# Sorting's constants ahead of the adjacency's transfers, node sums in two column tiles of the array, degrees within the table's chain

## The chip, the cores and the metric

The kernel runs on one core of one Trainium2 chip. The metric is the device time of one execution in microseconds (us), median of several runs. Profiles are of one execution each. In them PE is TensorE's matmuls, PEld its weight loads, DVE VectorE, ACT ScalarE, POOL GpSimd, SP SyncE. A releaser in square brackets after a line says how long the engine was idle before it and what ended that.

The change touches only what comes before the layer's last stage, 320.9 us in the kernel before. The rest, from the first product of that stage ("first mix product") to the end, is untouched.

## The reference, cut to what matters

Four graph layers follow one another; only the first is concerned. For 8 samples, 2048 nodes, 64 groups (H) and 64 features:

```python
h = x @ W
s = leaky_relu(h @ a_node, 0.2)
alpha = softmax(where(H.T > 0, s[:, None, :], NEG))        # over the nodes of a group
agg = einsum('ben,bnf->bef', alpha, h)                      # the node sums
beta = sigmoid((h @ a_gn)[:, None, :] + (agg @ a_ge)[:, :, None])
all_he = elu(beta * h + (1 - beta) * agg)                   # per node and group
deg = maximum(adj.sum(-1), 1.0)                             # degrees
industry = einsum('nm,bmf->bnf', adj / deg, x @ W_ind)
se = attn_scores(elu(agg))                                  # tanh(f @ fcW + fcb) @ av
g = einsum('bne,benf->bnf', softmax(where(H > 0, se, NEG)), all_he)
out = softmax-weighted sum of industry and g
```

The kernel sorts the nodes by their number of groups, so that a tile of 128 sorted nodes needs only as many "slots" (one group of each node at a time) as its fullest node.

## The kernel before

Its start has four parts. The 14.7 MB of the adjacency's first fourteen tiles are requested on GpSimd's queue. The sort runs on VectorE with small products on TensorE. The **node loop** makes, for each of 16 node tiles, h, the scores, the node sums in `pagg`, and a row block `st` which is written to HBM (`hs_hbm`) for the later gather in sorted order. The **table's chain** turns `pagg` into the table of groups and the one-hots of the first slots. Then the **slot loop** runs, one product of three passes (`pz`) per slot, with passes over the adjacency as filler: the degrees (`du`), then the layer's neighbour sums (`ug`).

```python
for t in range(NT - XT):                         # 14 of 16 adjacency tiles, 1 MB each
    ahead = min(t + 4, XB - 1)
    tc.keep_in_program_order(nc.gpsimd.tensor_copy(seen_x, xt[ahead][:, 0, 0:1]))
    load_adj(t)                                  # a transfer on GpSimd's queue
# ... only then on GpSimd:
nc.gpsimd.iota(iota, [[1, P]], base=0, channel_multiplier=0, ...)     # the sort's constants
# ... the sort on VectorE, then
nc.gpsimd.dma_start(av_col, ...)                 # and the other small transfers
for t in range(NT):                              # the node loop
    # ph = x tile by weights; seen, lr, e_gn
    st = pa.tile([P, HROW], F32, tag="st", name="st", bufs=5)
    nc.scalar.copy(st[:, BF + 8:], slot[:, t, :])
    # ... VectorE fills st and ex
    nc.scalar.dma_start(hs_hbm[t * P:(t + 1) * P, :], st)
    for k in range(2):
        nc.tensor.matmul(pagg[:, k, ...], lhsT=m_n[:, t, :], rhs=ex[:, k], ...)   # 64 groups
# ... the chain, with 40 of the 64 degree passes within it
def begin(t):                                    # slot loop, per tile
    both = split(hy, hrow[:, 0:BF], "hr", 2, [P, BF], pin=t < 2)      # hrl on VectorE
    # scores of the slots, then
    nc.vector.tensor_reduce(rs, ps[...], AX.X, ALU.add)
    nc.vector.tensor_scalar(rs, rs, 1.0e-30, None, op0=ALU.max)
    nc.vector.reciprocal(rs, rs)
```

Of the kernel before, what the change touches and what calls it, by code (L numbers as in the profile page):

```python
# [49 lines left out]
BINS = 16  # L50
# [6 lines left out]
def tile_gnn_fast(  # L57
# [151 lines left out]
    def staged(name):  # L209
        return hy.tile([P, JT, P], F32, tag="x", name=name, bufs=4)  # L210
# [5 lines left out]
    inv_row = hy.tile([P, N], F32, name="inv_row")  # L216
# [41 lines left out]


# [4 lines left out]
    with tc.tile_pool(name="pa", bufs=1) as pa, tc.tile_pool(name="pa_ps", bufs=1, space=PSUM) as pps:  # L264
# [5 lines left out]
        m_en = [pa.tile([P, HROW], F32, tag="st", name=f"m_en{c}", bufs=5)[0:E, 0:C] for c in range(NCH)]  # L270
# [9 lines left out]
        for t in range(XB):  # L280
            fetch_xt(t)

        bd66 = pa.tile([P, 2, F + 2], F32, name="bd66")
        nc.vector.memset(bd66, 0.0)
        w0t = pa.tile([F, P], F32, name="w0t")
        a2 = pa.tile([F, 2], F32, name="a2")
# [8 lines left out]
        for t in range(NT - XT):  # L295
            ahead = min(t + 4, XB - 1)
            tc.keep_in_program_order(nc.gpsimd.tensor_copy(seen_x, xt[ahead][:, 0, 0:1]))
            load_adj(t)
# [8 lines left out]
        tri = pa.tile([P, P], BF16, name="tri")  # L307
        make_upper_triangular(nc, tri, 1.0, diag=False)
        ones_b = pa.tile([P, P], BF16, name="ones_b")
        nc.vector.memset(ones_b, 1.0)  # L310
        iota = pa.tile([P, P], F32, name="iota")
        nc.gpsimd.iota(iota, [[1, P]], base=0, channel_multiplier=0, allow_small_or_imprecise_dtypes=True)
        row = pa.tile([P, 1], F32, name="row")
        nc.gpsimd.iota(row, [[1, 1]], base=0, channel_multiplier=1, allow_small_or_imprecise_dtypes=True)
        nc.vector.tensor_scalar(m_n, m_n, 0.0, None, op0=ALU.is_gt)
        deg = pa.tile([P, NT], F32, name="deg")
# [4 lines left out]
        oh = pa.tile(bins, BF16, name="oh")  # L321
        nc.vector.tensor_tensor(oh, deg[:, :, None].to_broadcast(bins), i16, ALU.is_equal)
        gt = pa.tile(bins, F32, name="gt")
        nc.vector.tensor_tensor(gt, deg[:, :, None].to_broadcast(bins), i16, ALU.is_gt)
        gts = pa.tile([P, BINS], F32, name="gts")
        nc.vector.tensor_reduce(gts, gt.rearrange("p t b -> p b t"), AX.X, ALU.add)
        gtb = pa.tile([P, BINS], BF16, name="gtb")
# [17 lines left out]
        rank = pa.tile([P, NT], F32, name="rank")  # L345
# [4 lines left out]
        caps = pa.tile([P, BINS], F32, name="caps")  # L350
        for s in range(BINS):
            nc.gpsimd.memset(caps[:, s:s + 1], float(P * SLOT_TILES[s]) if s < len(SLOT_TILES) else 0.0)
        over = pa.tile([P, BINS], F32, name="over")
# [5 lines left out]
        tri_e = pa.tile([E, E], BF16, name="tri_e")  # L359
        make_upper_triangular(nc, tri_e, 1.0, diag=True)  # L360
# [14 lines left out]
        tl = pa.tile([P, NT], F32, name="tl")  # L375
        ge = pa.tile([P, NT, NT], F32, name="ge")
# [7 lines left out]
        q = pa.tile([P, NT], F32, name="q")  # L384
# [4 lines left out]
        val = pa.tile([P, NT, 2, NT], BF16, name="val")  # L389
# [5 lines left out]
        for t in range(NT):  # L395
            ohq = pa.tile([P, P], BF16, tag="ohq", name="ohq", bufs=2)
            nc.vector.tensor_scalar(ohq, iota, q[:, t:t + 1], None, op0=ALU.is_equal)
            nc.tensor.matmul(
                po.rearrange("p i t -> p (i t)"), lhsT=ohq,
                rhs=val[:, t].rearrange("p i t -> p (i t)"), start=t == 0, stop=t == NT - 1,  # L400
            )
        olo = pa.tile([P, NT], F32, name="olo")
# [3 lines left out]
        for dst, v in ((fcb_col, fc_b), (av_col, av)):  # L406
            nc.gpsimd.dma_start(dst, v.rearrange("(n o) -> n o", o=1))
        for t in (fcz, bd_ind):
            nc.gpsimd.memset(t, 0.0)
        for b in range(2):  # L410
            s = slice(b * F, (b + 1) * F)
            nc.gpsimd.dma_start(fcz[s, b, :], fc_w)
            nc.gpsimd.dma_start(bd_ind[s, s], w_ind)
        nc.gpsimd.memset(avz, 0.0)
# [3 lines left out]
        age = pa.tile([E, F], F32, name="age")  # L418
        nc.gpsimd.dma_start(age, bass.AP(tensor=a_ge.tensor, offset=a_ge.offset, ap=[[0, E], [1, F]]))
# [3 lines left out]
        pagg = pps.tile([E, 2, C], F32, tag="agg", name="pagg", bufs=1)  # L423
        G = B // 2
        for t in range(NT):
# [8 lines left out]
            st = pa.tile([P, HROW], F32, tag="st", name="st", bufs=5)  # L434
# [22 lines left out]
            for k in range(2):  # L457
                nc.tensor.matmul(
                    pagg[:, k, 0:G * (F + 1)], lhsT=m_n[:, t, :], rhs=ex[:, k].rearrange("p g c -> p (g c)"),
                    start=t == 0, stop=t == NT - 1,  # L460
                )
# [14 lines left out]

        ones_r = hy.tile([P, P], F32R, name="ones_r")
        nc.gpsimd.tensor_copy(ones_r, ones)
        du = [pph.tile([P, 2, C], F32, tag="ph", name=f"du{g}", bufs=2) for g in range(2)]

        def degrees():
            for t in range(NT):
                for c in range(NCH):
                    mm(
                        du[c // 2][:, c % 2, :], lhsT=ones_r, rhs=adj[t][:, cols(c)],
                        start=t == 0, stop=t == NT - 1,
                    )
                    yield

        degree_passes = degrees()  # L490

        def some_degrees(tiles):
            for _ in range(tiles * NCH):
                next(degree_passes)

        some_degrees(6)


        gv = pagg[:, :, 0:G * (F + 1)].rearrange("p k (g c) -> p k g c", c=F + 1)
        den = pa.tile([E, B], F32, name="den")  # L500
        d3 = den.rearrange("p (k g) -> p k g", k=2)
        nc.vector.tensor_scalar(d3, gv[:, :, :, F], 1.0e-30, None, op0=ALU.max)
        nc.vector.reciprocal(den, den)
        agg = pa.tile([E, B, F], F32, tag="ex", name="agg", bufs=2)
        nc.vector.tensor_tensor(
            agg.rearrange("p (k g) f -> p k g f", k=2), gv[:, :, :, 0:F],
            d3[:, :, :, None].to_broadcast([E, 2, G, F]), ALU.mult,
        )
        tab = pa.tile([E, B, F], F32, tag="st", name="tab", bufs=5)
        tsm = pa.tile([E, 2, B], F32, name="tsm")  # L510
        sc = pa.tile([E, 2, B], F32, name="sc")
        nc.vector.tensor_tensor(tab, agg, age[:, None, :].to_broadcast([E, B, F]), ALU.mult)
# [4 lines left out]
            tab, agg, 1.0, tsm[:, 0, :, None].to_broadcast([E, B, F]), op0=ALU.add, op1=ALU.mult  # L517
        )
        tabf = tab.rearrange("p b f -> p (b f)")
        nc.scalar.copy(tab2[0:E, :], tabf)  # L520
        nc.vector.tensor_tensor(tab2[E:P, :], tabf, tab2[0:E, :], ALU.subtract)
        he = pa.tile([E, B, F], F32, tag="ex", name="he", bufs=2)
        nc.scalar.activation(he, agg, AF.Exp)
        nc.vector.tensor_scalar(he, he, -1.0, None, op0=ALU.add)
        nc.vector.scalar_tensor_tensor(he, agg, 0.0, he, op0=ALU.max, op1=ALU.min)
        pht = pps.tile([P, NP, E], F32, tag="sm", name="pht", bufs=2)
        for p in range(NP):
            tc.keep_in_program_order(nc.tensor.transpose(
# [26 lines left out]
    def load_x(dst, p, c):  # L555

        nc.sync.dma_start(dst, x_n[p, c])
# [1336 lines left out]
```

## Time and profile before

| | us |
|---|---|
| time, median of 3 (range) | 2263.1 (2261.5 to 2263.7) |
| VectorE's first operation that needs `iota` | 36.3 |
| first `st` of the node loop | 60.2 |
| T0: node sums done, degree passes begin | 98.7 |
| first slot product `pz` | 116.8 |
| TensorE streams without gaps from | 122.6 |
| last slot product | 308.2 |
| first mix product | 320.9 |

The lines that these come from stand in the prediction. In the view of busy time by stretch, a stretch is followed by its length, then by busy time and count of instructions of PE, PEld, DVE, ACT and POOL, then by the clock granted to TensorE (1.00 is full), by the share of the DMA engines and by GB/s.

### The profile page before, as it was taken

To read this page: it belongs to the slowest core of one execution; us is meant where nothing else is said; L and a number is where in the kernel's file an instruction comes from. 1 tells how busy PE (TensorE), PEld (TensorE's weight loads), DVE (VectorE), ACT (ScalarE), POOL (GpSimd) and SP (SyncE) were. 2 spreads that over 40 slices of the span, in tenths; PEclk is the share of its full clock that TensorE was granted. 3 is DMA by queue.
4 is the path that set the end of the run, shared out by engine and by line. 5 is a ranking of instruction groups with operands and counts; after the bars stand their busy time and mean duration, and the time that the engine had idled before them with its cause. 6 is when DMAs were issued, how large, how long until landed. Compare 5 with 4: busy or idle time off the path is not lost. (4 is left out here: it accounts for less than half of the span.)

```text
span 2256.9 us, 19846 instructions
## 1 busy us (share of the span) xinstructions
PE 1981.6 (88%) x7330; PEld 1279.6 (57%) x7330; DVE 1138.0 (50%) x1875; ACT 373.6 (17%) x684; POOL 538.3 (24%) x505
## 2 busy tenths in 40 slices
PE   1899978988858999889999999999986998989994
PEld 1578744655653444365456456447444786767773
DVE  1668967566633223215864772782884233332422
ACT  0223224223201111011010001001001111212210
POOL 3166557555322323200110110110010010010102
PEclk9989988999978999989999999999998999999997
DMA  9413233222220000010000000000001101111110
GB/s 347 161 40 91 83 116 102 70 86 73 68 52 0 19 19 19 0 42 5 7 8 3 7 10 0 10 8 3 7 7 32 47 24 52 38 47 47 45 31 21
DMA packets 65707, 104.31 MB, mean 46 GB/s; under 512 B 27312, under 2 KB 27360, under 8 KB 63360
## 3 DMA queue, kind: packets, MB, share of 16 engines
q1 hardware_dynamic: 54432, 70.51, 10.4%
q0 software_dynamic: 5856, 25.88, 3.5%
q10 hardware_dynamic: 5312, 6.56, 0.9%
q8 instruction: 60, 0.98, 0.2%
q14 instruction: 47, 0.39, 0.1%
HBM read 76.11 MB, written 26.80 MB: 46 GB/s over the span
## 5 line engine op out<-in xcount | busy, mean ns | idle before, releaser
L1013 PE MATMUL py<-wp,xg 128*128 128x512 f32 x1024 | 448.6, 597 | 8.5 <-DVE fcav L1018 5.9
L1013 PEld LDWEIGHTS py<-wp,xg 128*128 128x128 f32 x1024 | 193.6, 191 | 254.5 <-issue 216.0
L177 PE MATMUL u<-adj,hi 128*128 128x512 f32 x768 | 256.4, 415 | 0.0
L177 PE MATMUL u<-adj,lo 128*128 128x512 f32 x768 | 247.1, 401 | 0.0
L960 PE MATMUL u<-pt,xn 128*128 128x512 f32 x512 | 230.4, 609 | 8.3 <-DVE u L969 7.1
L1018 DVE TENSOR_TENSOR fcav<-py,emb_n 128x512 f32<-128x512 f32 x256 | 177.1, 692 | 52.0 <-PE py L1013 37.1
L1019 DVE TENSOR_REDUCE r<-fcav 128x32 f32<-128x512 f32 x256 | 175.5, 685 | 8.1
L1021 POOL TENSOR_TENSOR r<-r,bias 128x256 f32<-128x256 f32 x32 | 23.4, 730 | 636.2 <-DVE r L1019 636.2
L960 PEld LDWEIGHTS u<-pt,xn 128*128 128x128 f32 x512 | 98.3, 195 | 132.0 <-issue 116.9
L570 PE MATMUL u<-adj,vh 128*128 128x512 f32 x512 | 158.8, 409 | 14.7 <-ACT vh L168 10.9
L177 PEld LDWEIGHTS u<-adj,hi 128*128 128x128 f32 x768 | 143.2, 190 | 40.9 <-issue 11.0
L177 PEld LDWEIGHTS u<-adj,lo 128*128 128x128 f32 x768 | 145.0, 190 | 34.0
L570 PE MATMUL u<-adj,vl 128*128 128x512 f32 x512 | 152.3, 399 | 0.0
L156 POOL TENSOR_TENSOR ln_r<-ln_e,neg_half 128x8 f32<-128x8 f32 x64 | 106.5, 1664 | 168.7 <-DVE ln_e L154 168.0
L954 DVE TENSOR_SCALAR pt<-pt 128x512 f32<-128x512 f32 x64 | 48.8, 780 | 176.6 <-ACT pt L953 175.1
L1109 DVE SCALAR_TENSOR_TENSOR fcav<-fcav,ar 128x512 f32<-128x512 f32 x64 | 44.3, 692 | 174.5 <-ACT ar L1108 174.3
L1091 POOL TENSOR_TENSOR r<-r,xn 128x512 f32<-128x512 f32 x16 | 20.5, 1280 | 431.4 <-DVE r L1090 431.4
L570 PEld LDWEIGHTS u<-adj,vh 128*128 128x128 f32 x512 | 96.4, 190 | 45.0 <-ACT vh L168 12.4
L958 POOL TENSOR_TENSOR acc<-acc,pt 128x512 f32<-128x512 f32 x60 | 79.6, 1326 | 165.5 <-DVE pt L954 162.7
L570 PEld LDWEIGHTS u<-adj,vl 128*128 128x128 f32 x512 | 96.7, 190 | 22.3 <-issue 0.7
L150 ACT ACTIVATE r<-ln_c 128x512 f32<-128x512 f32 x64 | 40.4, 631 | 264.6 <-DVE ln_c L146 254.7
L755 POOL DMA_INDIRECT gn<-gs_hbm,rank x64 | 70.3, 1099 | 36.6 <-PE pg L180 16.9
(333 smaller groups left out, 2766.3 us busy)
## 6 DMA issues: line engine op xcount, KB each, us to landing
adj<-in_adj_t POOLq DMA_DIRECT2D x16, 1024.0 KB
fcav<-in_adj_t SPq DMA_DIRECT2D x64, 256.0 KB
x_hbm<-r SPq DMA_DIRECT2D x20, 256.0 KB
hs_hbm<-st ACTq DMA_DIRECT2D x16, 292.0 KB
xt<-in_x_t SPq DMA_DIRECT2D x16, 256.0 KB
xc<-in_x_n SPq DMA_DIRECT2D x16, 256.0 KB
u_hbm<-ut SPq DMA_DIRECT2D x16, 256.0 KB
gs_hbm<-acc SPq DMA_DIRECT2D x16, 256.0 KB
```

The costliest lines, as they stand in the source:

```text
L150: nc.scalar.activation(r, xc, AF.Square)
L156: nc.gpsimd.tensor_tensor(rstd, vare, neg_half[:, :groups], ALU.pow)
L177: tc.keep_in_program_order(nc.tensor.matmul(*args, **kw))
L570: nc.tensor.matmul(u[c], lhsT=half[:, j, :], rhs=adj[t][:, cols(c)], start=t == 0 and i == 0, stop=ends and not own,)
L755: nc.gpsimd.indirect_dma_start(out=gn[:, j, :], out_offset=None, in_=g_rows, in_offset=bass.IndirectOffsetOnAxis(ap=rank4[:, p, c * JT + j ...
L954: nc.vector.tensor_scalar(pt, pt, 1.0, None, op0=ALU.max)
L958: nc.gpsimd.tensor_tensor(acc, acc, pt, ALU.add)
L960: nc.tensor.matmul(u[p], lhsT=xn[p][:, t, :], rhs=pt, start=t == 0, stop=t == NT - 1)
L1013: nc.tensor.matmul(py.rearrange("p o d -> p (o d)"), lhsT=xg[b][:, q, cols(j, P)], rhs=wp[:, q, cols(k)], start=q == 0, stop=q == 1,)
L1018: nc.vector.tensor_tensor(pr, py, e_b, ALU.mult)
L1019: nc.vector.tensor_reduce(r[:, j, b, cols(k, OH)], pr, AX.X, ALU.add)
L1109: nc.vector.scalar_tensor_tensor(a, a, 1.0, ar.bitcast(F32), op0=ALU.mult, op1=ALU.not_equal, accum_out=left[:, t, k:k + 1],)
```

## The change

Its intent: the sort should not wait for constants and small transfers that stand behind the adjacency on GpSimd; `pagg` should use both halves of the array's columns (two groups of 64 output rows beside each other) instead of one half twice; all degree passes move into the table's chain, which then works on 128 partitions, and the slot loop loses work on VectorE.

```diff
+        iota = so.tile([P, P], BF16, name="iota")          # ahead of the adjacency
+        nc.gpsimd.iota(iota, ...)
+        # tri, row, caps, tri_e, and the transfers of fc_b, av, fc_w, w_ind, a_ge likewise
         for t in range(NT - XT):
-            ahead = min(t + 4, XB - 1)
-            tc.keep_in_program_order(nc.gpsimd.tensor_copy(seen_x, xt[ahead][:, 0, 0:1]))
+            if t in (0, 1):
+                tc.keep_in_program_order(nc.gpsimd.tensor_copy(seen_x, xt[2 * t + 1][:, 0, 0:1]))
             load_adj(t)
...
-            st = pa.tile([P, HROW], F32, tag="st", name="st", bufs=5)
+            st = pa.tile([P, HROW], F32, tag="st", name="st", bufs=4)
-                    pagg[:, k, 0:G * (F + 1)], lhsT=m_n[:, t, :], ...
+                    pagg[k * E:(k + 1) * E, 0:G * (F + 1)], lhsT=m_n[:, t, :], ...
...
-        ones_r = hy.tile([P, P], F32R, name="ones_r")
-        nc.gpsimd.tensor_copy(ones_r, ones)
-        some_degrees(6)                                    # later 2 and 2: 40 passes
+        ones_r = ta.tile([P, P], F32R, name="ones_r")
+        nc.vector.tensor_copy(ones_r, ones)
+        filler = products()                                # splits x (v0 to v3) first
+        fill(24)                                           # later 14, 14 and 12: 64 passes
...
-    pdc: 32 matmuls of one column                          # degrees into columns
+    pdc: 4 transposes of 128 columns
...
-    both = split(hy, hrow[:, 0:BF], "hr", 2, [P, BF], pin=t < 2)
+    both = split(..., nc.vector if t == 0 else nc.gpsimd, t == 0)
-    nc.vector.tensor_scalar(rs, rs, 1.0e-30, None, op0=ALU.max)
-    nc.vector.reciprocal(rs, rs)                           # one reciprocal for both now
```

## The prediction

> **What bounds the kernel now.** I read the page first: TensorE is busy 88% of the span and the hollow slices lie at the start, so I asked for busy time by stretch. Columns: span, then busy us and instructions of PE, PEld, DVE, ACT, POOL, then clock, DMA share, GB/s.
>
> ```profile
> 20.00:40.00 20.00, 3.26 (x35) 2.87 (x35) 2.54 (x11) 0.00 (x0) 7.98 (x39) 1.00 1.07 420
> 40.00:60.00 20.00, 3.52 (x16) 3.42 (x17) 4.12 (x21) 1.43 (x9) 4.26 (x10) 0.66 0.79 298
> ...
> 240.00:260.00 20.00, 19.74 (x90) 15.60 (x88) 18.48 (x34) 6.43 (x14) 13.10 (x14) 1.00 0.25 82
> ```
>
> Up to 60 us only the transfers are full (420 GB/s); nearly every engine waits. The slot loop (117 to 315 us) is the opposite: TensorE bound, VectorE close behind. Everything from 315 us on is untouched by the change, so the question is how much earlier that point comes. VectorE's order of time says what it waits for:
>
> ```profile
> 36.26 0.42 DVE L322 TENSOR_TENSOR oh<-deg,iota 128x256 bf16<-128x256 f32 x1 [23.06 <-POOL iota L312]
> ...
> 57.40 0.30 DVE L417 COPY fcav<-av_col 128x64 f32<-128x64 f32 x2 [15.88 <-DMA av_col<-in_av]
> ```
>
> Two waits, 39 us. The sort's iota stands on GpSimd's queue behind 14 adjacency transfers; then av_col (issued at 40.17) lands only behind them. From 57.6 to 98.8 the rest of the sort and the node loop run (2.12 us per tile on TensorE, VectorE idle 0.32 of it). Then the table's chain:
>
> ```profile
> 98.70 5.79 PE L177 MATMUL du<-adj,ones_r 128*128 128x512 f32 x24
> ...
> 116.77 0.77 PE L177 MATMUL pz<-hrh,ident_r 128*128 128x512 f32 x1
> ```
> ```profile
> 108.87 7.54 POOL L254 TENSOR_SCALAR o<-slot 128x128 fp32r<-128x128 bf16 x12 [4.52 <-ACT slot L250]
> ```
>
> Call T0 the end of the node sums, 98.8. The twelve one-hots start at T0+10.1, end at T0+17.6, and the first slot product is at T0+18.0: GpSimd's one-hots end this chain. The second tile's scores finish at 122.7 (T0+24); from there TensorE streams.
>
> Last, who shares the transfers. From 18 to 20 us (queue: packets, MB, share):
>
> ```profile
> q0 software_dynamic: 85, 0.63, 80.0%
> q1 hardware_dynamic: 95, 0.17, 26.2%
> ```
>
> Beside the adjacency (q0, 7.4 KB a packet) SyncE's queue (q1, 1.8 KB) gets some 80 GB/s, packet for packet.
>
> **What the Trainium skill says.** "DMA: Bandwidth & Descriptors", "Queues, rings and completion order": each engine goes round robin between queues, packet by packet. The trace agrees (95 packets against 85 above). "TensorE: Matmul & The Clock Gate", part 3, "Packing small matmuls": matmuls on different tiles of the array run concurrently, 2.38 times for three column tiles; the kernel before has no pair of column tiles, so its trace cannot say. "GPSIMD Engine Reference", "Key points": it shares its SBUF interfaces with VectorE, which contends in two-port modes or with two SBUF inputs. The trace agrees: a 128x8 tensor_scalar takes 0.16 us alone but 0.94 on average in the slot loop, once 4.10:
>
> ```profile
> L169 DVE TENSOR_TENSOR hrl<-hrow,hrh 128x512 fp32r<-128x512 f32 x16 | 18.0, 1123 | 0.3 <-ACT hrh L168 0.3
> L675 DVE TENSOR_SCALAR rs<-rs 128x8 f32<-128x8 f32 x16 | 15.1, 941 | 0.0
> ```
>
> "Part 1: The HAM clock gate" of the TensorE page: the clock halves after idle windows; here it was 0.50 from 117 to 127 us, after the idle chain.
>
> **Part 1, constants first.** iota and tri are made by about 2.5 us, the small transfers issued by 8.7 (the same instructions, 7.5 us of GpSimd). VectorE's oh then needs only what stands before it in its order, which ends at 13.2: 23 us earlier. av_col, on an empty queue, lands before the 18.6 at which it is wanted: the 15.9 us go too. Taken alone: T0 at 98.8 - 39 = 60.
>
> But two things take part of this back. (a) The instruction order of the changed kernel puts two casts, v0h and v1h, on ScalarE in front of the first st<-slot, so the node loop waits for xc0 and xc1. These stand on SyncE's queue behind m_n and eight xt: 0.52 + 8 x 0.26 + 2 x 0.26 = 3.15 MB. The adjacency now starts without the staggered waits, issued at 8.7, moving at about 11 (2 us after issue, as before). By 11 q1 has moved 1.75 MB (from the stretches before); the other 1.4 at 80 GB/s take 17.5 us, plus 1 to 2 for the slowest ring: about 30. First st at about 31.7 against 60.17: 28.5 us gained, not 39. (b) Adjacency 14.7 MB, xt 8 to 15 2.1 MB, the rest of q1 1.4 MB and the node rows' writes (hs) 4.8 MB now compete: 23 MB from 11 us at 420 GB/s is 55 us, to 66. st has 4 buffers instead of 5, and a write beside two other busy queues gets about 80 GB/s, 3.8 us per 0.3 MB. I reckon 2 us lost to this at the end.
>
> **Part 2, node sums in column tiles.** In a tile the four pagg passes take 1.09 of 2.12 us. Packed they should take about 0.55; VectorE's 1.80 us per tile then bounds. About 12 tiles x 0.32 = 4 us.
>
> T0 = 98.8 - 28.5 - 4 + 2, near 69: 30 us earlier.
>
> **Part 3, degrees in the chain.** All 64 du passes now stand before the loop, 24 more than before. TensorE by its order: du 24 5.8, pht 0.45, du 14 3.5, pf 1.0, du 14 3.5, pslot 0.3, du 12 3.0, pse 0.6: T0+18.1; the halved table shortens only VectorE and ScalarE work that is hidden. The one-hots decide: in GpSimd's order v0l to v3l stand before them, v2l and v3l need v2h and v3h, and ScalarE has those behind its two copies of the finished degrees (du ends at T0+17.5). So: copies to T0+18.7 (0.6 each), v2h and v3h to 19.9, v2l and v3l (1.3 each) to 21.9, twelve one-hots (7.54) to 29.4, first product at T0+30: 12 later than T0+18.0. Next five one-hots after a row fetch (1.07 + 3.1) and five scores: streaming from T0+34 against T0+24. Cost: 10 us. Streaming begins near 103 against 122.7: 20 us earlier.
>
> **Part 4, slot loop.** VectorE loses hrl (15 of 16 moved to GpSimd), rs max and one reciprocal: 17 + 15 + 3 = 35 us of 148 busy between 145 and 310. TensorE, idle 7 us there, becomes the sole bound; I give it 4 to 5 back. GpSimd gains 15 x 1.29 = 19 us, has room (13 of 20), and follows. The 24 du passes are 5.5 us less TensorE work (0.228 each), but the loop asks for 558 passes of filler (9 a slot, 3 a tile) and 512 are left instead of 536, so it runs out about slot 52 of 57 instead of 55; the last five then go at VectorE's pace, about 2.5 us instead of 3.1. Of 5.5 I keep 2. Sum: 6 to 7.
>
> **Sum.** -20 - 6.5 = -26.5 at the end of layer 0, kept to the end: 2263 - 26 = 2237 us.
>
> **The rivals.**
> 1. The chain isn't lengthened (the v splits come early enough, or the streamed degrees are worth their full 5.5 us): 10 us better, 2226. Against it: the orders above, which are fixed. With T0 at 62 as well, 2218.
> 2. The transfers become the bound of the node loop: if the writes are starved until the adjacency has ended and eight or more tiles then follow at 2 us, T0 is 75 to 80 and the time about 2245. For it: the transfers were already full from 20 to 55 us. Against it: packets are shared evenly, and 4 buffers keep a write waiting all the time.
> 3. GpSimd becomes the loop's bound, hrl being late for a tile's first product, above all in the last six tiles, of two slots or one. There it has 4.9 us of work per tile (fetch 1.06, one-hots 1.26, hrl and acc 1.29 each) against TensorE's 6.2. It would cost up to 8 us: 2245.
> 4. The gain is hidden: not possible for a wait that every later stage stands behind; 315 us is reached with no other engine or transfer ahead of the loop.
>
> **Range and chances.** The start's gain lies between 24 and 37, the chain's loss between 0 and 13, the loop's gain between 0 and 9; not all extreme together: 2224 to 2250. Over 2% faster means below 2217.9, 45 us, which needs rival 1 in full: 0.08. Slower by 2% has no mechanism: 0.01.
>
> **What would show it.** Right: VectorE's oh at 13 to 14 us with no wait on iota; ScalarE's first st<-slot after v1h near 30; pagg 0.55 us per tile; T0 near 69; the one-hots starting some 22 us after T0, after v3l; first pz some 30 after T0; VectorE at 70 to 75% in the loop, TensorE without idle until the filler ends; the stages after the loop as long as before. Wrong: st<-slot near 20 (then (a) falls), T0 above 75 (rival 2), one-hots within 12 us of T0 (rival 1), TensorE waiting for hrl (rival 3), or pagg still at 1.09.

## The result, and the profile after

| | before | predicted | after | after, control run |
|---|---|---|---|---|
| time, median | 2262.7 | 2237 | 2233.2 (2227.1 to 2235.3) | 2234.2 |
| ratio, 95% interval | | | 0.9865 (0.9844 to 0.9886) | 0.9886 (0.9870 to 0.9903) |
| first `st` | 60.2 | 31.7 | 28.2 | 26.3 |
| T0 | 98.7 | 69 | 80.4 | 78.8 |
| first slot product | 116.8 | 99 | 108.5 | 106.9 |
| streaming | 122.6 | 103 | 112.4 | 110.8 |
| last slot product | 308.2 | | 281.3 | 279.8 |
| first mix product | 320.9 | 294.4 | 294.5 | 292.9 |

A ratio is the mean time of one kernel's fast runs over that of the other's of the same rounds, so not quite the ratio of the medians quoted; 2262.7 is the median of the first table's three runs and one more. The control is the changed kernel run once more, with the second batch of experiments.

The end came 26.4 us earlier at the first mix product, where the prediction had 26.5. But the milestones between show that it came about otherwise. The waits of the sort went as foreseen. VectorE's order of time, the changed kernel:

```profile
17.42 0.42 DVE L421 TENSOR_TENSOR oh<-deg,iota 128x256 bf16<-128x256 f32 x1
22.58 0.29 DVE L502 COPY fcav<-av_col 128x64 f32<-128x64 f32 x2
28.20 0.42 DVE L536 SCALAR_TENSOR_TENSOR st<-ph,st 128x256 f32<-128x256 f32 x1 [4.46 <-ACT st L529]
```

Neither `oh` nor the copy of `av_col` has a wait any more (23.06 and 15.88 us before). `st` waits 4.46 us for ScalarE. ScalarE's own order of time shows why, and what came after it:

```profile
26.85 0.62 ACT L168 CAST v1h<-xc 128x512 fp32r<-128x512 f32 x1 [2.53 <-DMA xc<-in_x_n]
...
36.56 0.24 ACT L527 CAST st<-slot 128x64 f32<-128x64 bf16 x1 [4.67 <-DMA hs_hbm<-st]
45.41 0.24 ACT L527 CAST st<-slot 128x64 f32<-128x64 bf16 x1 [7.73 <-DMA hs_hbm<-st]
53.54 0.24 ACT L527 CAST st<-slot 128x64 f32<-128x64 bf16 x1 [5.51 <-DMA hs_hbm<-st]
```

The cast `v1h` in front is the predicted step (a). The lines below it are the news: the node loop now stops again and again until the write of an earlier `st` has left its buffer. These waits are 25 us in sum, and the last is at 62.7. Meanwhile the transfers are full, as the busy time by stretch shows:

```profile
20.00:40.00 20.00, 12.63 (x66) 8.59 (x65) 10.87 (x47) 3.13 (x13) 2.66 (x5) 0.66 1.07 417
40.00:60.00 20.00, 13.82 (x62) 9.18 (x61) 8.44 (x29) 2.10 (x11) 0.00 (x0) 0.59 1.06 410
60.00:80.00 20.00, 16.95 (x100) 11.42 (x100) 14.79 (x44) 4.97 (x26) 0.00 (x0) 0.82 0.38 149
```

In these three stretches VectorE is busy 10.9, 8.4 and 14.8 of 20 us, so the loop runs at its own pace only in the third, when the transfers have fallen to 149 GB/s. Who gets the 410 GB/s between 40 and 50 us (queue: packets, MB, share; q0 is the adjacency, q1 SyncE's x tiles, q10 the writes)?

```profile
q0 software_dynamic: 441, 3.20, 79.8%
q1 hardware_dynamic: 286, 0.52, 15.8%
q10 hardware_dynamic: 177, 0.38, 10.2%
```

The writes get 0.38 MB in 10 us, 38 GB/s. The prediction had counted on 80. But this is a mean, and not the share of a write whose rows are moving. From 39 to 40 us of the control (the changed kernel once more) all three queues have rows to move. A packet is then one row: 8 KB of the adjacency, 2 KB of x, 2.3 KB of a node row block.

```profile
q0 software_dynamic: 33, 0.27, 66.8%
q1 hardware_dynamic: 32, 0.07, 19.6%
q10 hardware_dynamic: 32, 0.07, 18.8%
```

Here the queues move row for row, and the writes have 75 GB/s, near the 80. The mean is lower for two other reasons, both read from the control's trace. First, a write stands before it moves: the first five took 7.7 to 10.0 us from issue to landing, 3.5 to 5.8 of them before their first row, where those after 64 us, alone in the queues, took 2.1 and 0.8 (medians). Second, few writes are under way, until 62 us never more than two. ScalarE issues them in its own order, and a write that is ready stands there behind the copy `st<-slot` of a later tile, which waits for a buffer. The third row block was ready at 39.3. VectorE's last operation on it, and ScalarE's copy for the sixth tile with the third tile's write behind it:

```profile
38.86 0.42 DVE L536 SCALAR_TENSOR_TENSOR st<-ph,st 128x256 f32<-128x256 f32 x1
...
43.97 0.24 ACT L527 CAST st<-slot 128x64 f32<-128x64 bf16 x1 [8.18 <-DMA hs_hbm<-st]
44.03 0.33 ACTq L543 DMA_DIRECT2D hs_hbm<-st  x1
```

The fifth lost 4.8 us in the same way (ready at 47.1, issued at 52.0). In the first run of the changed kernel, TensorE's order of time shows the node sums in a starved and in a free stretch, then T0 and the first slot product:

```profile
47.50 1.14 PE L545 MATMUL pagg<-ex,m_n 128*64 128x260 f32 x4 [1.90 <-DVE ex L540]
...
72.37 0.66 PE L545 MATMUL pagg<-ex,m_n 128*64 128x260 f32 x4
...
80.43 5.87 PE L177 MATMUL du<-adj,ones_r 128*128 128x512 f32 x24
...
108.46 0.77 PE L177 MATMUL pz<-hrh,ident_r 128*128 128x512 f32 x1
```

The column tiles bring the four passes from 1.09 to 0.66 us, but only at the full clock; in the starved stretch (clock 0.59 above, 0.50 from 47 to 49 us) they take 1.14. The chain is longer than before, 28.0 us from T0 to the first slot product against 18.1, for the predicted reason; GpSimd's order:

```profile
98.27 1.26 POOL L169 TENSOR_TENSOR v2l<-xc,v2h 128x512 fp32r<-128x512 f32 x1 [9.32 <-ACT v2h L168]
99.49 1.27 POOL L169 TENSOR_TENSOR v3l<-xc,v3h 128x512 fp32r<-128x512 f32 x1
100.73 7.37 POOL L255 TENSOR_SCALAR o<-slot 128x128 fp32r<-128x128 bf16 x12
```

GpSimd waits 9.32 us for `v2h`, which ScalarE makes behind its copies of the finished degrees; only then come `v2l`, `v3l` and the twelve one-hots.

In the slot loop, finally, two things were not in the prediction. The start of the loop by stretch, first of the kernel before, then of the changed one:

```profile
122.70:130.00 7.30, 7.30 (x21) 5.75 (x21) 6.69 (x9) 0.51 (x1) 4.66 (x4) 0.60 0.56 151
```
```profile
112.40:120.00 7.60, 7.60 (x36) 6.26 (x37) 4.92 (x10) 0.60 (x1) 4.65 (x3) 1.00 0.13 39
```

TensorE is busy throughout in both, but did 21 instructions at a clock of 0.60 before and 36 at 1.00 after. And the step that turns the degrees into columns, again before, then after:

```profile
137.70 3.73 PE L177 MATMUL pdc<-ones,inv_row 1*128 1x1 f32 x32
```
```profile
116.20 0.60 PE L180 MATMUL pdc<-ident,deg 128*128 128x128 f32 x4
```

`hrl`, which VectorE made before, shows in the groups of the loop as GpSimd's, with 0.6 us of idle time before it in all, 0.4 of it for `hrh`; `rs`'s maximum (15.1 us of VectorE) is gone:

```profile
L169 POOL TENSOR_TENSOR hrl<-hrow,hrh 128x512 fp32r<-128x512 f32 x15 | 20.7, 1382 | 0.6 <-ACT hrh L168 0.4 <-DVE ut L333 0.2
```

So the theory to be tested was: **T0 is late because the adjacency's outstanding transfers starve the writes of the node rows, not because the loop starts late; and the slot loop gained more than predicted, which hid it.** The rival for T0: it is the start of the loop, the casts or the four buffers that cost. The rival within the theory: it isn't a matter of shares; the same 23 MB have to land in any case.

### The profile page after: what moved, and what is told of

Read it like the earlier page. It is cut to its first block, busy times and chain, and to the rows that moved or that the text cites. A ratio compares the mean times of both kernels' runs of the same rounds, so it can differ in the third digit from the quotient of the medians.

```text
span 2233.5 us, 19741 instructions
## 1 busy us (share of the span) xinstructions
PE 1979.0 (89%) x7292; PEld 1279.6 (57%) x7292; DVE 1115.8 (50%) x1833; ACT 374.7 (17%) x688; POOL 553.8 (25%) x507
## 5 line engine op out<-in xcount | busy, mean ns | idle before, releaser
L1028 POOL TENSOR_TENSOR r<-r,bias 128x256 f32<-128x256 f32 x32 | 23.3, 729 | 636.2 <-DVE r L1026 636.2
L645 PE MATMUL u<-adj,vh 128*128 128x512 f32 x512 | 158.8, 409 | 14.7 <-ACT vh L168 10.9
```

Of the source, the lines that this page charges most:

```text
L645: nc.tensor.matmul(u[c], lhsT=half[:, j, :], rhs=adj[t][:, cols(c)], start=t == 0 and i == 0, stop=ends and not own,)
```

## The experiments

Twelve runs followed, one of them the changed kernel again; all gave correct results. The milestones of all of them, in us (T0 is the first degree pass; "streaming" is where the second tile's scores end, with TensorE without gaps from there; "st waits" is the sum of ScalarE's waits for the writes; "clock" is where the granted clock becomes full, worked out from the granted share in stretches of 2 us):

| run | first st | st waits | T0 | first pz | streaming | clock | last pz | mix product | time | ratio to before |
|---|---|---|---|---|---|---|---|---|---|---|
| before | 60.2 | 1 | 98.7 | 116.8 | 122.6 | 128.5 | 308.2 | 320.9 | 2262.7 | |
| after | 28.2 | 25 | 80.4 | 108.5 | 112.4 | 111.7 | 281.3 | 294.5 | 2233.2 | 0.9865 |
| control | 26.3 | 27 | 78.8 | 106.9 | 110.8 | 109.7 | 279.8 | 292.9 | 2234.2 | 0.9886 |
| e1 | 22.9 | 34 | 88.6 | 108.2 | 113.6 | 119.3 | 299.1 | 311.8 | 2250.9 | 0.9958 |
| e2 | 27.2 | 25 | 79.3 | 101.0 | 108.8 | 113.7 | 279.9 | 293.0 | 2234.1 | 0.9888 |
| e3 | 23.3 | 30 | 76.4 | 105.5 | 109.6 | 114.8 | 280.9 | 294.0 | 2231.1 | 0.9871 |
| e4 | 26.4 | 27 | 77.7 | 106.0 | 110.0 | 114.8 | 287.6 | 300.4 | 2236.3 | 0.9899 |
| e5 | 26.8 | 31 | 77.9 | 105.9 | 110.0 | 113.6 | 280.6 | 293.8 | 2237.3 | 0.9885 |
| e6 | 28.3 | 21 | 81.3 | 109.3 | 113.4 | 117.4 | 284.1 | 297.3 | 2227.1 | one run |
| e9 | 25.4 | 19 | 70.8 | 106.7 | 110.7 | 114.0 | 281.2 | 294.4 | 2236.7 | 0.9885 |
| e10 | 26.1 | 23 | 74.8 | 101.0 | 105.0 | 108.5 | 275.1 | 288.5 | 2231.7 | 0.9879 |
| e11 | 25.2 | 16 | 65.4 | 101.7 | 105.7 | 110.6 | 276.6 | 289.8 | 2227.8 | 0.9851 |
| e12 | 32.9 | 20 | 78.8 | 106.8 | 110.9 | 115.8 | 281.8 | 295.0 | 2234.9 | 0.9883 |
| e13 | 25.3 | 28 | 70.3 | 99.9 | 103.4 | 103.2 | 272.1 | 285.3 | 2221.5 | 0.9826 |

The 95% intervals of the ratios are 0.002 to 0.003 on each side. The intervals of e2, e3, e4, e5, e9, e10 and e12 overlap the control's widely, that of e11 slightly (0.9822 to 0.9879 against 0.9870 to 0.9903); what these runs say, their milestones say.

### Control: the changed kernel once more

> The changed kernel once more, unedited, as a control on this chip: e2, e3 and e4, which equal it up to the degree passes except for e3's transfers, showed T0 at 79.3, 76.4 and 77.7 against 80.4, and the clock full only 5 us after streaming began, where the changed kernel's trace had it full at once. Theory (both vary from run to run): T0 77 to 81, half clock for up to 5 us at the start of streaming, first mix product at 294 to 297. Rival (the changed kernel has them by its order): T0 80 to 81 and the clock full when streaming begins.

T0 was 78.8 and the first mix product 292.9, a us below what was expected. The clock was full when streaming began, as in the first run; in e5, e6, e9 and e12, which have the same instructions there, it was full only 3.3 to 4.9 us later. The Trainium skill, "TensorE: Matmul & The Clock Gate", "Part 1: The HAM clock gate", says that the activity window is free-running, so that the cold stretch varies from run to run; these runs agree, and 5 us at half clock are 2.5 us of work lost. So T0 is good to 1 or 2 us and the start of the loop to 2.5.

### e1: the constants alone

```diff
--- before
+++ e1: the constants and small transfers moved up, nothing else
+        nc.gpsimd.iota(iota, ...)  # and tri, row, caps, tri_e, av_col, fc_b, ...
         for t in range(NT - XT):
             ...
             load_adj(t)
-        nc.gpsimd.iota(iota, ...)
```

> The kernel before with one part of the change alone: the sort's constants and the small transfers stand ahead of the adjacency's transfers on GpSimd. The chain, the loop, st's 5 buffers, the order of the casts and the staggered start of the adjacency stay as before. Theory (the transfers starve the node loop once it starts early): VectorE's oh moves from 36.3 to about 17 and the wait for av_col goes, but ScalarE's st<-slot then waits for the node rows' own writes for 15 us and more in sum, and T0, the start of the degree passes, comes at about 80 instead of 98.8; first slot product at T0+18 as before; time 2263 - 18 = 2245. Rival (removing the waits is worth what they lasted, 39 us, and what the changed kernel missed is due to its casts and its 4 buffers): T0 60 to 65, time 2225 to 2230.

The first `st` came at 22.9, 37 us earlier than before and without a cast in front, with five buffers, with the adjacency's staggered start. All the same the loop stood for 34 us in sum and the node sums ended at 82.3. So the waits need neither the casts nor the fourth buffer nor the missing stagger; the rival falls. (In this run the last of the 14 adjacency tiles landed at 67.6, in the control at 61.5: the end of the node sums went with the adjacency, not with the start.) A second finding was not foreseen. TensorE's order of time:

```profile
88.62 1.65 PE L177 MATMUL du<-adj,ones_r 128*128 128x512 f32 x3 [6.33 <-POOL ones_r L478]
```

The degree passes waited 6.33 us for the cast `ones_r`, which stands on GpSimd behind two row fetches and two adjacency transfers. The change has that cast on VectorE, a line that the prediction had passed over. What the changed kernel would lose without it was not run. In e1 it is 6.3 of the 8.6 us by which T0 came later than the expected 80; the rest is the end of the node sums, 82.3. The total gained 9 us and not 18.

### e2: v2 and v3 split later

```diff
--- changed kernel
+++ e2
-        for c in range(NCH):
+        for c in range(2):
             fetch(0, c); parts(0, c)
...
+                    if p == 0 and g == 0 and t in (0, 3):      # within the first mix pass
+                        fetch(0, 2 + t // 3); parts(0, 2 + t // 3)
```

> The changed kernel, but the splits of the third and fourth quarter of x (v2, v3) are emitted within the first mix pass instead of before the degree passes, so that GpSimd's twelve one-hots don't stand behind v2l and v3l. Theory (these two splits and what they wait for lengthen the chain): the one-hots start at about T0+14 instead of T0+20.3, the first slot product comes at T0+22 to T0+23 instead of T0+28; the next one-hots, of the second tile, then stand behind v2l and v3l, which gives back 2 to 4; time 2 to 5 us below the changed kernel. Rival (the chain's length is set by TensorE's degree passes and not by GpSimd): first slot product at T0+27 or later and the time that of the changed kernel.

The first slot product came at T0+21.7, as the theory had it. But the total stayed. GpSimd's order shows where it went:

```profile
93.56 7.10 POOL L255 TENSOR_SCALAR o<-slot 128x128 fp32r<-128x128 bf16 x12 [5.70 <-ACT slot L251]
...
102.01 1.33 POOL L169 TENSOR_TENSOR v2l<-xc,v2h 128x512 fp32r<-128x512 f32 x1
103.24 1.31 POOL L169 TENSOR_TENSOR hrl<-hrow,hrh 128x512 fp32r<-128x512 f32 x1
104.47 1.30 POOL L169 TENSOR_TENSOR v3l<-xc,v3h 128x512 fp32r<-128x512 f32 x1
105.70 2.77 POOL L255 TENSOR_SCALAR o<-slot 128x128 fp32r<-128x128 bf16 x5
```

The second tile's five one-hots now stand behind the two splits and `hrl`. Streaming began at T0+29.5 instead of T0+32.0, and 5 us of it ran at half clock. Of 6.3 us at the first product, 1.5 were left at the mix product against the first run of the changed kernel and none against the control. The splits do lengthen the chain, but what counts is the second tile.

### e3: small pieces of the adjacency

```diff
-        tc.keep_in_program_order(nc.gpsimd.dma_start(adj[t], adj_t[t * P:(t + 1) * P, :]))
+        for c in range(NCH):
+            tc.keep_in_program_order(nc.gpsimd.dma_start(adj[t][:, cols(c)], adj_t[t * P:(t + 1) * P, cols(c)]))
```

> The changed kernel, but each adjacency tile is fetched by four transfers of 512 columns (2 KB rows instead of 8 KB). Theory (the queues take turns packet by packet, so the adjacency's large packets starve the node rows' writes and x): at 20 to 40 us the adjacency's queue has no more than half of what is moved instead of some 80%, v1h is cast at 18 to 21 instead of 26.9, the waits of st<-slot for the writes fall from 26 us in sum to under 12, T0 comes at 62 to 70 instead of 80.4, and the time falls by 10 to 18 us. Rival (23 MB at 420 GB/s end near 66 us in whatever order, and the loop can't end before): T0 stays within 4 us of 80, the time within 4 us of the changed kernel's.

`v1h` was cast at 22.0, a us later than hoped. But T0 was 76.4, only 2.4 us before the control's, and the waits were 30 us in sum. The queues from 30 to 40 us:

```profile
q0 software_dynamic: 1813, 3.30, 108.4%
q10 hardware_dynamic: 144, 0.30, 8.1%
q1 hardware_dynamic: 159, 0.29, 8.0%
```

Rows are now about 2 KB on all three queues. The 144 packets are one write, 128 rows and 16 packets of 4 bytes; no other was under way. The smaller pieces shorten a write, to between 5.6 and 7.2 us for the first twelve, but 2.8 to 3.7 us of them still pass before its first row. So the size of the adjacency's rows isn't what makes a write wait. From 40 to 50 us the writes had 0.90 MB, more than double the changed kernel's, but the adjacency still moved 1.98 MB from 60 to 70 us, and the last wait for a write was at 69.8 instead of 62.7. The rival (the same bytes have to land in any order) describes T0 better.

### e4: the slot loop's relief undone

```diff
-            both = split(..., nc.vector if t == 0 else nc.gpsimd, t == 0)
+            both = split(..., pin=t < 2)                    # hrl on VectorE
+            nc.vector.tensor_scalar(rs, rs, 1.0e-30, None, op0=ALU.max)
+            nc.vector.reciprocal(rs, rs)                    # and its own reciprocal
```

> The changed kernel with the slot loop's relief of VectorE undone: hrl on VectorE, the sum's maximum and a second reciprocal back. Theory (VectorE's relief is worth only TensorE's idle time that it removed, 6.2 to 2.1 us; the rest of the loop's gain comes from fewer degree passes, the transposes in place of 32 one-column matmuls, and the granted clock at its start): the stretch from the start of streaming to the first mix product becomes 4 us longer (180 against 176), the time 4 us longer. Rival A (it is worth all of the 10 us by which the loop gained more than predicted): 10 us or more. Rival B (worth nothing): within 1 us of the changed kernel's loop.

From streaming to the last slot product it took 177.6 us. Taking off half of the 4.8 us that the clock was halved leaves 175.2. The same sum for the runs whose loop is the changed kernel's (after, control, e5, e6, e9, e12) gives 168.4 to 169.0, in the middle 168.8. So the relief of VectorE is worth 6.4 us: more than the 4 to 5 of the prediction, less than rival A's 10. The first mix product was 5.9 us later than the changed kernel's although T0 had been 2.7 earlier. The total is 2 to 3 us longer, within the intervals. (The expectation's 176 us from streaming to the mix product is 182.1 by these milestones.)

### e5: the casts late

```diff
-            part[c] = split(hy, xc.pop((p, c)), f"v{c}", 1, [P, JT, P], nc.gpsimd)
+            part[c] = split(hy, ..., nc.gpsimd, p == 0 and c < 2)   # keeps v0h, v1h behind the node loop
```

> The changed kernel with the casts v0h and v1h kept in program order, so that they stand behind the node loop on ScalarE instead of ahead of its first st<-slot. Theory (the transfers bind the node loop, not its start): first st at 22 to 24 instead of 28.2, the waits of st<-slot for the node rows' writes grow by about as much, T0 within 2 us of the control. Rival (step (a) of the prediction: each us of a later first st is a us of T0): T0 4 to 5 us earlier than the control's.

ScalarE's first `st<-slot` moved to 23.0, but the first `st` stayed at 26.8, since VectorE did more of the sort in front of it. My expectation of 22 to 24 was wrong. The waits grew by 5 us, and T0 was 77.9, 0.9 before the control. So the place of the casts costs T0 1 us at most; but since the first `st` did not move, the run doesn't say what an earlier start is worth. That a late start is not why T0 missed the predicted 69 follows from the first run: its `st` came at 28.2, 3.5 us earlier than predicted. (A fifth buffer for `st` in the changed kernel was not tested; e1 has five.)

### e9: a paced adjacency

```diff
-        for t in range(NT - XT):
+        for t in range(4):
...                                                    # in the node loop, behind tile t's scores
+            for a in {1: (4,), 4: (5,), 7: (6,), 10: (7,), 12: (8,), 13: (9,), 14: (10,), 15: (11, 12, 13)}.get(t, ()):
+                tc.keep_in_program_order(nc.gpsimd.tensor_copy(seen_x, seen[:, t, 0, 0:1]))
+                load_adj(a)
```

> As e5, and in addition GpSimd issues only the first four adjacency transfers ahead of the node loop; five more follow one by one, each behind a copy of a node tile's scores (tiles 1, 4, 7, 10, 12), and the others behind tiles 13 to 15. Theory (the node loop is starved because 14.7 MB of adjacency are outstanding at once; it needs only 7 MB itself): the waits of st<-slot for the writes fall from 26 us in sum to under 6, the node loop runs at about 1.9 us a tile, T0 comes at 54 to 60, the chain from there is as long as before (28 to 32), and the time is 15 to 25 us below the control. Rival (the same 23 MB have to land before the degree passes can end, so that what T0 gains is lost in them): T0 near 60, but TensorE waits for the adjacency within the degree passes, first slot product not before 100, time within 8 us of the control.

T0 came at 70.8, 8 us before the control's; the first slot product came 0.2 us before it. The rival was right about the degree passes and the time. T0 near 60, which theory and rival both had, was missed by 11 us, and the waits were 19 us and not under 6. A single outstanding adjacency tile is enough to hold a write up: one issued at 56.2, behind a tile issued at 55.7, moved its first row at 60.3 and landed at 63.1. From 56 to 60 us (q10's packets are the end of the write before):

```profile
q0 software_dynamic: 99, 0.81, 79.7%
q10 hardware_dynamic: 39, 0.05, 3.6%
```

And what T0 gained was lost where the degree passes waited for the last tiles, as TensorE's order shows:

```profile
90.19 2.04 PE L177 MATMUL du<-adj,ones_r 128*128 128x512 f32 x4 [3.88 <-DMA adj<-in_adj_t]
```

Between 30 and 40 us the transfers had been at 162 GB/s, because the next tile's turn had not come. Bytes not moved then were missing at 90.

### e10: the same with GpSimd's order mended

```diff
+            if t <= 1:                                 # one-hots of both first tiles in program order
                 tc.keep_in_program_order(made)
+        # v2 and v3 split in program order within the first mix pass, behind both
```

> As e9, and GpSimd's order in the chain mended: v2 and v3 are split within the first mix pass and only after the one-hots of the second tile, which are kept in program order too (e2 had only the first tile's one-hots ahead of them and gave the gain back at the second tile's). Theory: first slot product at T0+22, streaming from T0+27 instead of T0+32, so 4 to 5 us below e9. Rival (the second tile's rows or the degree passes decide by then): within 2 us of e9.

Streaming began at 105.0 instead of e9's 110.7 and the mix product came 5.9 us earlier: the mended order is worth what was expected. In distances from T0 it was less (T0+26.2 and T0+30.2 instead of 22 and 27), because the degree passes took 20.2 us instead of the changed kernel's 16.4: they began at half clock and waited 1.65 us for the adjacency. The total's interval overlaps with e9's.

### e11: eight tiles ahead, eight behind

```diff
-        for t in range(NT - XT):
+        for t in range(8):
...
         fetch_rows(0)
         fetch_rows(1)
-        for t in range(NT - XT, NT):
+        for t in range(8, NT):
             load_adj(t)
```

> The changed kernel, but only eight of the adjacency's sixteen tiles are asked for ahead of the node loop; the other eight are issued after it, behind the first two row fetches, so that none of them can stand before a node row's write. The casts are late as in e5 and GpSimd's order is mended as in e10. Theory (any adjacency transfer outstanding holds the writes up: in e9's trace the writes moved 0.05 MB in a stretch of 4 us in which the adjacency moved 0.81; and the degree passes can't end before the last adjacency tile): the waits of st<-slot end by about 40, the loop then runs at 1.85 us a tile, T0 comes at 56 to 62, the last adjacency tile at 80 to 84, the last degree pass just behind it, and streaming begins at 86 to 92 instead of 110.8 in the control; time 15 to 22 us below it. Rival (as in e9: the transfers lose as much to idle stretches as the loop gains): streaming not before 103, time within 8 us of the control.

This shows the starving most plainly. With half the adjacency outstanding, the last of it landed at 41.6 and the waits ended at 43.4, from where the loop ran at 1.8 to 1.9 us a tile, and in the stretch from 40 to 60 us a write took 2.2 us from issue to landing. T0 came at 65.4, 13 us before the control's (expected: 56 to 62). But the last degree passes waited for the adjacency until 94.5, where I had expected the last tile at 80 to 84: between 40 and 70 us the transfers ran at 245, 185 and 112 GB/s. Streaming began at 105.7. The theory is right about what delays T0; the rival is right for the time, 6.4 us below the control's, of which 3.1 show at the mix product.

### e12: each write on two queues

```diff
-            nc.scalar.dma_start(hs_hbm[t * P:(t + 1) * P, :], st)
+            nc.scalar.dma_start(hs_hbm[t * P:t * P + half, :], st[0:half])
+            nc.sync.dma_start(hs_hbm[t * P + half:(t + 1) * P, :], st[half:P])
```

> The changed kernel, but each node row block is written in two halves, 64 rows from ScalarE's queue and 64 from SyncE's. Theory (the queues take turns, so that two of them get twice the share): the waits of st<-slot for the writes fall from 26 us in sum to under 18, T0 comes 4 to 7 us before the control's 78.8. Rival (writes stand behind the adjacency's transfers whichever queue they come from, or the x tiles on SyncE's queue lose what the writes gain): T0 within 2 us of 78.8 or later.

T0 was 78.8, the control's to 0.1 us. The sum of the waits was lower only because the loop started later (v0h's data landed 6.6 us later in this run; why is open). The Trainium skill, "DMA: Bandwidth & Descriptors", "Rules for kernel authors", advises against two transfers for disjoint partition halves, since both run on the same 16 engines; the run agrees. With the first `st` at 32.9 against 26.3 and the same T0, either the start of the loop doesn't matter or the split gained what the late start cost; this run can't tell. Only half of each write was freed from ScalarE's order: the third tile's halves were issued at 44.6 and at 51.1. A write issued wholly elsewhere, or `st<-slot` taken off ScalarE, was not tried.

### e13: what the runs point to

```diff
+        for t in range(6):  ...                        # six tiles ahead
+        # from node tile 3 on, two pieces of 128 x 512 behind each tile's scores: six more tiles
+        for t in range(12, NT): load_adj(t)            # four behind the row fetches
...
+        slots(0, pps, "sm", 2)                         # right after the table's first product
+        slots(1, pps, "sm", 2)
         fill(14)
```

> The changed kernel rearranged by what e9 to e11 showed: six adjacency tiles ahead of the node loop; six more in pieces of 128 x 512 (0.26 MB), two behind the scores of each node tile from the fourth on, so that a piece holds the writes up for well under 1 us; the last four behind the first two row fetches. Casts late as in e5. The first two tiles' slots are transposed right after the table's first product, so that GpSimd's seventeen one-hots run beside the degree passes; v2 and v3 are split after them. Theory: the waits of st<-slot end by 40, T0 at 60 to 64, the last adjacency tile at 76 to 81, the last degree pass just behind it, first slot product 6 us later, streaming at 84 to 89 instead of 110.8 in the control, and the time 18 to 25 us below the control's: 0.978 to 0.981 of before. Rival (the pieces hold the writes up as whole tiles did, or the rows of the first tiles arrive late behind them): T0 over 66, streaming after 97, time less than 12 us below the control's.

It is the fastest of all, 2221.5 us, 0.9826 (0.9806 to 0.9846) of before; this interval lies apart from the control's 0.9870 to 0.9903, though not from e11's, and it touches that of the first run (0.9844 to 0.9886). At the mix product it is 7.6 us before the control, in the total 12.7; the rest is the untouched stages. But the way there was not the expected one. T0 was 70.3 and streaming began at 103.4, which are the rival's numbers. The pieces do hold the writes up (28 us of waits), and 44% busy transfers from 70 to 80 us, while the row fetches waited for the last writes, were missing at the last degree pass:

```profile
91.24 2.08 PE L177 MATMUL du<-adj,ones_r 128*128 128x512 f32 x4 [1.71 <-DMA adj<-in_adj_t]
```

What helped was the chain: from the last degree pass at 93.3 it was 6.6 us to the first slot product, against 11.7 in the changed kernel (96.8 to 108.5). It is not the early one-hots that shorten it, since e10 and e11 have 6.0 us without them; all three have the splits of `v2` and `v3` behind the one-hots. Against e10 and e11 the degree passes ended 1.7 and 2.4 us earlier and the clock was full 5 and 7 us earlier.

### e6: the node sums made twice

```diff
+            for k in range(2):
+                nc.tensor.matmul(pagg_x[k * E:(k + 1) * E, ...], lhsT=m_n[:, t, :], rhs=ex[:, k], ...)
```

> The changed kernel with each node tile's four column-tile passes of pagg made once more, into a spare bank of PSUM (its result is unused): TensorE has again what the kernel before had for them, 1.3 us a tile instead of 0.66. Theory (part 2 counts only for the tiles that are left when the writes flow, six or seven of sixteen): the distance between node tiles after 65 us rises from 1.85 to 2.3 to 2.5, before it nothing changes, T0 comes 3 to 4 us later than the control's 78.8. Rival (VectorE sets the pace in any case, the column tiles are worth nothing): distance 1.85 and T0 as in the control.

The order of time on TensorE:

```profile
67.51 0.66 PE L546 MATMUL pagg<-ex,m_n 128*64 128x260 f32 x4
68.00 0.61 PE L551 MATMUL pagg_x<-ex,m_n 128*64 128x260 f32 x4
...
69.63 0.66 PE L546 MATMUL pagg<-ex,m_n 128*64 128x260 f32 x4
```

The distance between tiles is 69.63 - 67.51 = 2.12 us, exactly that of the kernel before, less than the 2.3 to 2.5 expected. So in the free stretch the column tiles are worth 2.12 - 1.85 = 0.27 us a tile, for the eight tiles after 61 us 2.2 us together. T0 at 81.3 is 2.5 after the control's but 0.9 after the first run's, so it confirms nothing. Before 60 us the writes set the pace, and a shorter pass gains nothing.

## Why the prediction was right or wrong

**The time was right, its path wasn't.** The sum had four terms; measured at the milestones of the first run they are:

| term | predicted | measured |
|---|---|---|
| T0 earlier | 30 | 18.3 |
| chain to streaming longer | 10 | 8.1 |
| streaming earlier | 20 | 10.2 |
| slot loop shorter | 6.5 | 16.7 |
| end of the layer earlier | 26.5 | 26.4 (mix product), 26.8 (last slot product) |

**Constants first: right.** Both waits went. `oh` was at 17.4 instead of 13.3, because a small product in front waited for its own load until 16.3, and `v1h` at 26.9 instead of 30. That the first `st` decides T0 was wrong, however: it came 3.5 us earlier than predicted and T0 11 us later, and in e11 it came 1.1 us before the control's and T0 13.

**Step (b), "I reckon 2 us lost to this at the end": the step that failed.** Had it held, T0 would have been at 98.7 - 32.0 (first `st` earlier) - 2.2 (column tiles) + 2 = 66.5. It was 80.4, so the contention cost 16 us. Two things in it were wrong, and the share of 80 GB/s was not one of them.

The first is a sum. At 80 GB/s a write takes 3.8 us, twice the loop's pace of 1.85 us a tile. Between the first `st` at 31.7 and 66 us nine writes can land so; with four buffers thirteen tiles have then begun, and three more at 1.85 us, with 5.7 us from the last tile's copy to T0 (74.7 to 80.4 in the first run), put T0 near 78. That is an estimate from the prediction's own figures and these two measured ones, 9 us above the 69 it wrote.

The second is "4 buffers keep a write waiting all the time". Writes were ready and not issued, up to 5 us long, because ScalarE stood in front of them waiting for the next buffer; and each write under way took 7.7 to 10.0 us and not 3.8, since 3.5 us or more passed before its first row. So with 14 tiles outstanding only eight of sixteen node tiles had been begun by 61 us. The other eight, and what stands in the pipeline behind them, followed at the loop's own pace in the 18.9 us up to T0. Rival 2 of the prediction described exactly this with T0 at 75 to 80; only the time it named (2245) was not reached, because of the loop.

What holds the writes up is settled in part. Outstanding adjacency transfers do it (e9, e11: without them a write takes 2.1 to 2.8 us). The waits come without the casts, with five buffers and with the stagger (e1), with small rows (e3) and with two queues (e12). Why so much time passes before a write's first row isn't shown, nor how the 16 us divide between that and ScalarE's order.

**Column tiles: mechanism right, size off.** 0.66 us instead of 0.55 at the full clock, and 0.27 us for eight tiles instead of 0.32 for twelve: 2.2 us instead of 4.

**The chain: right.** One-hots began at T0+20.3 and ended at T0+27.7 (predicted 21.9 and 29.4), behind `v3l`, as in the instruction order; the first product was at T0+28.0 (30). e2 confirms the cause at the first product and corrects its worth: what sets streaming is the second tile.

**The slot loop: mechanism right, mis-sized, and two terms missing.** Of 16.7 us, measured from streaming to the last slot product (185.6 against 168.9): VectorE's relief 6.4 (e4; predicted 4 to 5); `pdc` 3.73 - 0.60 = 3.1, which the prediction overlooked; the clock 4.4, also not in it, of which 3.0 (half of 5.9 us) at the start are partly chance and 1.4 (5 us at 0.72, from 140 to 145 us) lie about the one-column products; the rest, 2.8, is left for the 24 degree passes, of whose 5.5 us the prediction had kept 2. That split by subtraction is argued, not shown. The filler ran out earlier, as predicted: its last pass began 5.1 us before the last slot product, against 1.4.

**Rival 3** (GpSimd late with `hrl`) didn't happen: the loop's groups show no large wait on it. **Rival 4** had been excluded rightly: every us at the mix product reached the end, within the spread of the untouched stages.

The two errors, 12 us at T0 and 10 in the loop, cancelled by luck. A prediction of the same sum without milestones would have looked confirmed.

## What to carry to other kernels

Removing a wait moves work into a stretch in which the transfers may already be full, and then the stop only moves to the next buffer: before crediting the wait, add up the bytes that must have landed by the end of the stage. When a small transfer has to come out between large ones, hold back the issue of the large ones rather than split the small one or reorder what is outstanding; but a byte held back while the transfers idle is paid again by whoever needs it last. Buffers keep transfers under way only if the engine that issues them doesn't stand waiting, in its own order, for the next buffer. And check a prediction at its intermediate times, not only at the end.

## What the Trainium skill lacked or had wrong

- "DMA: Bandwidth & Descriptors", "Queues, rings and completion order": round robin between queues fits what the trace shows where all three have rows moving (33, 32 and 32 packets, 39 to 40 us of the control); the page counts several descriptors to a packet, where each of these packets is one row. It has no figure for how long a write stands before its first row beside another queue's loads: 3.5 us and more here against 0.8 alone, 2.8 to 3.7 with small rows (e3), and 4.1 behind a single tile of 1 MB (e9).
- "TensorE: Matmul & The Clock Gate", "Part 3: Packing small matmuls", has no measured figure for two column tiles of 64: here four passes of 260 columns took 0.66 us instead of 1.09, 1.65 times as fast, and 1.14 at half clock.
- "Part 1: The HAM clock gate" of the same page has no figure for what the varying cold stretch does to a loop like this: it began at full clock in two runs and 3.3 to 4.9 us late in four others (e5, e6, e9, e12), up to 2.5 us of work.
- "GPSIMD Engine Reference", "Key points", says that VectorE is about twice as fast in elementwise work: `hrl` alone is 0.69 us on VectorE and 1.29 on GpSimd, which agrees, but in the slot loop, where both work, it was 1.15 before (on VectorE) and 1.38 after (on GpSimd), 1.2 times.
